# A routed expert layer: the up product with its weights as the stationary side, fetched per tile from DRAM

## The chip, the cores and the metric

The kernel runs on one core of a Trainium2 chip. The metric is the device time of one launch in microseconds, the median over runs. The engines of the core are TensorE (PE, with its weight loads in a row of its own, PEld), VectorE (DVE), ScalarE (ACT), GpSimd (POOL) and SyncE (SP, which here only issues DMAs). All arithmetic is fp32. In this trace one fp32 product stands as two matmul records, a transpose as one.

## The reference, cut to what matters

The network takes `u` of shape (8, 512, 128) through eight residual blocks: a rotating state-space layer, a feed-forward layer, a four-layer linear-attention encoder, the feed-forward layer again, causal attention with its own feed-forward, a mixture of experts, a gated linear attention, and the mixture of experts once more with the same weights. Each block reads a layer norm of the stream and adds its result. The block that matters is the mixture of experts, with 8 experts, 128 features, 352 hidden units, and two experts for each token:

```python
xn = rms_norm(x, norm_scale)
scores = jnp.einsum('bsd,ed->bse', xn, w_router)
_, ids = jax.lax.top_k(scores, 2)
c = jnp.take_along_axis(jax.nn.softmax(scores, axis=-1), ids, axis=-1)
h = jnp.einsum('bsd,ehd->bseh', xn, w_up)          # 704 = 2 * 352 columns
val, gate = jnp.split(h, 2, axis=-1)
h = val * jax.nn.silu(gate)
y = jnp.einsum('bseh,edh->bsed', h, w_down)
yk = jnp.take_along_axis(y, ids[..., None], axis=2)
out = jnp.sum(yk * c[..., None], axis=2) + x
```

## The kernel before

All blocks are recorded into one list of operations, each with the engines that can do it, a planned cost, the operations it depends on and a rank. A planner in the kernel (`Flow.run`) then goes through the list: at each step it takes the operation that can start first by its own planned times, and of equals the one of lowest rank. The result is a fixed order on every engine, written out by `Flow.emit`. The rank of an operation is the age of its thread plus the TensorE cost that the thread has recorded so far (`f.turn(thread, age)`). So the three constants at the end, `FIRST` (ages of the eight sequences in the first five blocks), `LATER` and `AGES` (ages of the threads of the last three blocks), decide which thread goes first where several could. The lag of an operation is how long after its end the planner lets its readers start. SP's queue is ordered in the same way, and each engine works through its queue strictly in order.

The last three blocks work on two halves of four sequences each. For each half and each of the two mixtures there are four threads. *Enter* makes the normed rows, writes them to DRAM (`rows_in`) and computes the scores. *Route* (`moe_route`) sorts the 4096 token-expert pairs of the half into 39 tiles (`TILES`) of 128 rows, one expert for each tile, and leaves three lists of integers: `h.get` (the rows to gather), `h.put` (where each result goes) and `h.off` (the column at which the tile's expert begins). *Experts* (`moe_experts`) does the tiles, 156 in all four passes. *Combine* loads the scattered rows back (`moe_combine`, line 2091) and adds the two results of each token to the stream. Between the two mixtures stands the gated attention of the half (`gated_steps`).

A tile goes like this. An indirect DMA on POOL gathers 128 rows (line 1983). Four tiles are transposed into one PSUM bank, and one operation scales them into `xt`. `wide` reads the tile's offset into a register of TensorE and does two products with `xt` as the stationary side: the gate (line 2018) and the value (line 2019), each 352 columns wide, from the expert's weights, which all eight experts hold on chip in `room_m` (8 x 1088 words a partition: 704 up, 384 down). Tanh on ScalarE and two operations on VectorE make the activation `g`, 128 tokens by 352 units. Three transposes through the identity and one copy turn it into `gt`. `deep` (line 2028) does three products with `gt` as stationary side and the down weights moving, 128 columns each. After four tiles the result is scaled, and an indirect DMA on POOL scatters each tile's rows (line 1993). There are three buffers for `g` and two for `gt`, `xr`, `xt` and `yr`. Their names in the trace are only `left` and `right`, the two areas of SBUF, and nearly all operations are recorded at lines 216 and 231.

Of the kernel before, what the change touches and what calls it, by code (L numbers as in the profile page):

```python
# [12 lines left out]
I32 = mybir.dt.int32  # L13
AF = mybir.ActivationFunctionType
ALU = mybir.AluOpType
# [5 lines left out]
P = 128  # L21
B = 8
S = 512
D = 128
NT = S // P
HALVES = 2
# [3 lines left out]
TILES = (2 * B * S // HALVES + 8 * (P - 1)) // P  # L30
# [648 lines left out]
def f_copy(f, out, in_):  # L679
    f.either(("scalar", "copy", (out, in_), {}), ("vector", "tensor_copy", (out, in_), {}))  # L680
# [10 lines left out]
class EncLane:  # L691

    WORDS = 3968

# [127 lines left out]
class FrontLane:  # L822

    WORDS = 4136

# [923 lines left out]
class MoeLane:  # L1749

    N = HALVES * NT
    WORDS = 0

    def __init__(self, base, ints):
        n, e = B // HALVES * NT, 8
        lane = Lane(base)
        self.r, self.by = lane.take(8, n, e), lane.take(3, e, n)
        self.high = lane.take(2 * n, TILES, at=0)
        self.m, self.full, self.q = lane.take(8, n), lane.take(e, n), lane.take(4, e)
        self.c = lane.take(2, n)  # L1760
        self.own = self.by.rearrange("p a e t -> p (a e t)")[:, 0 : TILES * e].rearrange("p (i e) -> p i e", e=e)
        self.ex, self.src = lane.take(TILES), lane.take(TILES)
        self.bits = [(LnBits(lane), lane.take(2, NT), lane.take(NT)) for i in range(B // HALVES)]
        self.get, self.put = ints[:, 0:TILES], ints[:, TILES : 2 * TILES]
        self.off = ints[0:1, 2 * TILES : 3 * TILES]
        self.saves, self.gathers, self.puts, self.loads, self.written = [], [], [], [], []

    @staticmethod
# [5 lines left out]
class ExpertLane:  # L1774


    def __init__(self, base, xn, y, low):
        lane = Lane(base)
        self.xn, self.y, self.low = xn, y, low
        self.zt = [lane.take(S) for i in range(2)]  # L1780
        self.xr, self.xt = [lane.take(4, D) for i in range(2)], [lane.take(4, P) for i in range(2)]
        self.g, self.gt = [lane.take(3 * P) for i in range(3)], [lane.take(3, P) for i in range(2)]
        self.yr = [lane.take(4, D) for i in range(2)]
        self.turn = {}

    WORDS = 1024 + 2048 + 1152 + 768 + 1024

    def next(self, name):
        i = self.turn[name] = self.turn.get(name, -1) + 1
# [4 lines left out]
def scaled(f, out, in_, by):  # L1794
# [1 line left out]
        ("scalar", "activation", (out, in_, AF.Copy), dict(scale=by)),  # L1796
        ("vector", "tensor_scalar", (out, in_, by, None, ALU.mult), {}),
    )


def moe_ready(k, f, box):

    for g in box.g:
        f.gpsimd.memset(g, 0.0)


def moe_enter(k, f, w, b, h, box):
# [38 lines left out]
def moe_route(k, f, w, half, h, box):  # L1846
# [66 lines left out]
        ALU.is_ge,  # L1913
    )
    v.tensor_reduce(h.ex[0:1], h.own[0:1], AX.X, ALU.add)
    v.tensor_scalar(h.ex[0:1], h.ex[0:1], float(E - 1), float(ROW), ALU.min, ALU.mult)
    v.tensor_copy(off, h.ex[0:1])
    v.tensor_tensor(e, s, wide(0), ALU.subtract)
    f.scalar.activation(e, e, AF.Exp)
    v.tensor_reduce(m[:, 1, :], e, AX.X, ALU.add)  # L1920
# [51 lines left out]
def moe_experts(k, f, w, half, h, box):  # L1972

    HID, ROW, E = 352, 1088, 8
    nc, tc = k.nc, k.tc
    xs, ys, off = k.rows_in[half], k.rows_out[half], h.off
    before, saved, h.gathers, h.puts, h.saves = h.loads, h.saves, [], [], []
    k.turn_of += 1
    group, written = f"rows{k.turn_of}", []
    h.written = written  # L1980

    def get(x, i):
        return lambda: nc.gpsimd.indirect_dma_start(  # L1983
            out=x.real(),
            out_offset=None,
            in_=xs,
            in_offset=bass.IndirectOffsetOnAxis(ap=h.get[:, i : i + 1].real(), axis=0),
        )

    def put(y, i):  # L1990

        def emit():
            made = nc.gpsimd.indirect_dma_start(  # L1993
                out=ys,
                out_offset=bass.IndirectOffsetOnAxis(ap=h.put[:, i : i + 1].real(), axis=0),
                in_=y.real(),
                in_offset=None,
            )
            if written:
                tc.declare_no_dep(made.ins, group=group, reason="no two of them write the same row")  # L2000
                tc.add_manual_dep(made.ins, written[0].name, SYNC, reason="what it overwrites")
            tc.add_to_no_dep_group(group, made.ins)
            written.append(made.ins)

        return emit

    def wide(i, held, pg, pv, xt, experts):

        def emit():
            o = held[i] = nc.values_load(  # L2010
                off[0:1, i : i + 1].real(),
                engines=[mybir.EngineType.PE],
                min_val=0,
                max_val=(E - 1) * ROW,
                skip_runtime_bounds_check_because="clamped where it is made",
            )
            all_of = experts.real()
            nc.tensor.matmul(pg.real(), xt.real(), all_of[:, bass.ds(o + HID, HID)], start=True, stop=True)  # L2018
            nc.tensor.matmul(pv.real(), xt.real(), all_of[:, bass.ds(o, HID)], start=True, stop=True)  # L2019

        return emit

    def deep(i, held, py, gt, experts):

        def emit():
            o, all_of = held[i], experts.real()
            for q in range(3):
                nc.tensor.matmul(  # L2028
                    py.real(),
                    gt[:, q, :].real(),  # L2030
                    all_of[:, bass.ds(o + 2 * HID + q * D, D)],
                    start=(q == 0),
                    stop=(q == 2),
                )

        return emit

    held = {}
    experts = w["experts"]
    for first in range(0, TILES, 4):  # L2040
        m = min(4, TILES - first)
        xr, xt, yr = box.next("xr"), box.next("xt"), box.next("yr")
        for j in range(m):
            i = first + j
            h.gathers.append(
                f.op([("gpsimd", 1.26, get(xr[:, j, :], i), None)], [h.get[:, i : i + 1]], [xr[:, j, :]], after=saved, lag=2.2)
            )
        pt, py = f.ps([P, 4, P]), f.ps([P, 4, D])
        for j in range(m):
            f.tensor.transpose(pt[:, j, :], xr[:, j, :], k.ident)  # L2050
        scaled(f, xt[:, 0:m, :], pt[:, 0:m, :], k.col["m_ns"])
        for j in range(m):
            i = first + j
            g, gt = box.next("g"), box.next("gt")
            pg, pv = f.ps([P, HID]), f.ps([P, HID])
            f.op([("tensor", 1.27, wide(i, held, pg, pv, xt[:, j, :], experts), None)], [xt[:, j, :], off, experts], [pg, pv])
            f.scalar.activation(g[:, 0:HID], pg, AF.Tanh, scale=0.5)
            f.vector.scalar_tensor_tensor(g[:, 0:HID], g[:, 0:HID], 1.0, pg, ALU.add, ALU.mult)
            f.vector.tensor_tensor(g[:, 0:HID], g[:, 0:HID], pv, ALU.mult)
            pt = f.ps([P, 3, P])  # L2060
            for q in range(3):
                f.tensor.transpose(pt[:, q, :], g[:, q * P : (q + 1) * P], k.ident)
            f_copy(f, gt, pt)
            f.op([("tensor", 0.68, deep(i, held, py[:, j, :], gt, experts), None)], [gt, experts], [py[:, j, :]])
        if first + m < TILES:
            scaled(f, yr[:, 0:m, :], py[:, 0:m, :], 0.5)
        for j in range(m):
            i = first + j
            if first + m == TILES:
                scaled(f, yr[:, j, :], py[:, j, :], 0.5)  # L2070
            h.puts.append(
                f.op(
                    [("gpsimd", 1.26, put(yr[:, j, :], i), None)],
                    [yr[:, j, :], h.put[:, i : i + 1]],
                    [],
                    after=before + h.puts[:1],
                    lag=2.2,
                )
            )

# [296 lines left out]
def both_blocks(k, saved, out):  # L2377
# [6 lines left out]
    with tc.tile_pool(name="net", bufs=1) as one:  # L2384
# [97 lines left out]

        some, other = cut(left), cut(right)
        f.turn("load", -1000.0)
        room_m = some(8 * 1088)
        y = [shaped(some(4 * D), (2, 2, D)) for i in range(2)]
        room_g, room_head = some(2338), some(304)
        hs = [MoeLane(some(MoeLane.words()), some(3 * TILES + 3).bitcast(I32)) for i in range(HALVES)]
        rows = [shaped(some(NT * D), (NT, D)) for i in range(2)]
        room_x = some(ExpertLane.WORDS)  # L2490
        pairs = [GatedLane(other(GatedLane.WORDS)) for i in range(2)]
        kept = other(GATED_FOLD)
        low = [shaped(other(4 * P), (4, P)) for i in range(2)]
        w = f.load(k, "m", room_head, only=("wr", "rev", "before", "iota", "dest"))
        w |= f.load(k, "m", room_m, parts=8, only=("experts",))
        wg = f.load(k, "g", room_g)
        box = ExpertLane(room_x, rows, y, low)
        f.turn(("route", 0, True), LATER + AGES[0])
        moe_ready(k, f, box)

        age = [LATER + a for a in AGES]

        def moe(half, first, then, out=None):
# [38 lines left out]
            f.emit(tiles)  # L2542


LATER = 700.0


AGES = [-33.0, -19.0, -149.0, -22.0, 62.0, 85.0, 147.0, -119.0, 102.0, -157.0]


FIRST = [30.0, 66.0, 62.0, 89.0, 185.0, 190.0, 210.0, 220.0, 327.0]


@with_exitstack
# [275 lines left out]
```

## Time and profile before

| what | value |
|---|---|
| median of 9 runs (lowest to highest) | 1644.92 us (1641.38 to 1649.53) |
| the profiled execution: its time, its span | 1644.99 us, 1643.3 us |
| mean granted clock of TensorE | 0.976 |
| the two up products (lines 2018 and 2019), 312 records each | 479 and 469 ns mean of a record |
| the three down products (line 2028), 936 records | 279 ns mean of a record |
| indirect gathers and scatters on POOL | 156 each, mean 1002 and 1010 ns |
| gather, from its issue to landing | 2.6 us median (2.4 to 3.6) |
| DMA over the span | 54.26 MB, 33 GB/s |

The span runs from the first to the last instruction, and the profiled execution's own time is 1.7 us longer. A row of a group gives its engine, its operation, what it writes and reads, its count, its busy time, the mean of one in ns, and the idle time ahead of it with what ended that. TensorE's matmuls overlap and their ends are modelled, so the distance between starts says more than a duration. Idle time of an engine that is not the bound costs nothing.

### The profile page before, as it was taken

The page shows a single profiled execution, that of the slowest core. Times are in us where ns is not written, and L with a number is a line of the kernel's source. Part 1 is how long each engine was busy: PE and PEld are TensorE (multiplying, and loading weights), DVE is VectorE, ACT ScalarE, POOL GpSimd, SP SyncE. Part 2 cuts the span into 40 slices and gives each one's busy share as a digit, 9 for nine tenths or more (in the row PEclk, how much of TensorE's full clock was granted, in tenths as well). Part 3 has the DMA queues.
Part 4 walks back from the last instruction along what each step waited for, and adds up shares of the span by engine and source line. Part 5 has one row for each costly group of instructions (what it writes and reads, how often), then busy time and mean ns, then how long its engine had stood idle before and what let it go on. Part 6 is the DMA issues. An engine that isn't in the chain of part 4 may idle for free.

```text
span 1643.3 us, 29385 instructions
## 1 busy us (share of the span) xinstructions
PE 1554.2 (95%) x10231; PEld 1105.4 (67%) x10231; DVE 1095.2 (67%) x3413; ACT 926.1 (56%) x1824; POOL 839.3 (51%) x976
## 2 busy tenths in 40 slices
PE   4899999999999999999999999999999999999894
PEld 2567866767567576687566556787558875687773
DVE  7588656658756567567576753576986769976453
ACT  1466566556665656656667756545744357454452
POOL 4375344455444544435444465657245572556773
PEclk9899999999999999999999999999989999999997
DMA  6000000000000000001003010113001130012334
GB/s 222 1 1 1 1 1 8 2 1 8 1 1 8 1 8 1 1 19 44 1 28 108 14 26 28 43 38 99 14 20 38 37 99 14 20 40 44 83 95 104
DMA packets 40546, 54.26 MB, mean 33 GB/s; under 512 B 7012, under 2 KB 32101, under 8 KB 40135
## 3 DMA queue, kind: packets, MB, share of 16 engines
q1 hardware_dynamic: 21400, 26.62, 5.2%
q0 software_dynamic: 10256, 21.38, 5.1%
q10 hardware_dynamic: 8736, 4.29, 0.8%
q8 instruction: 86, 1.41, 0.4%
q14 instruction: 68, 0.56, 0.1%
HBM read 33.52 MB, written 18.61 MB: 32 GB/s over the span
## 4 chain that ended last, share of the span: by engine, by line


## 5 line engine op out<-in xcount | busy, mean ns | idle before, releaser
L216 PE MATMUL ps_w<-left 128*128 128x128 f32 (+3 forms) x2540 | 450.7, 322 | 7.0 <-DVE left L216 5.7
L216 PEld LDWEIGHTS ps_w<-left 128*128 128x128 f32 x2540 | 332.4, 193 | 100.0 <-issue 64.1
L216 PE MATMUL ps_w<-right 128*128 128x128 f32 (+2 forms) x1656 | 348.6, 351 | 20.6 <-DVE right L216 13.3
L216 PEld LDWEIGHTS ps_w<-right 128*128 128x128 f32 x1656 | 225.9, 196 | 97.3 <-issue 55.1
L216 ACT ACTIVATE right<-ps_w 128x512 f32<-128x512 f32 (+1 forms) x394 | 206.8, 597 | 92.3 <-PE ps_w L231 74.8
L216 ACT ACTIVATE left<-ps_w 128x352 f32<-128x352 f32 (+2 forms) x307 | 157.3, 519 | 137.0 <-PE ps_w L216 58.5
L216 ACT COPY left<-ps_w 128x384 f32<-128x384 f32 (+3 forms) x268 | 128.1, 489 | 163.8 <-PE ps_w L216 141.2
L231 PE MATMUL ps_w<-right 128*32 128x512 f32 (+9 forms) x2256 | 202.7, 444 | 9.0 <-DVE right L216 5.6
L216 DVE SCALAR_TENSOR_TENSOR left<-left,ps_w 128x352 f32<-128x352 f32 (+1 forms) x220 | 122.7, 563 | 124.7 <-ACT left L216 124.1
L1993 POOL DMA_INDIRECT rows_out<-left x156 | 157.6, 1010 | 80.4 <-ACT left L216 38.2
L1983 POOL DMA_INDIRECT left<-rows_in,left x156 | 156.3, 1002 | 66.8 <-issue 28.9
L216 PE MATMUL ps_w<-w_ident,left 128*128 128x128 f32 x1072 | 178.1, 282 | 6.3 <-DVE left L216 4.1
L216 DVE TENSOR_TENSOR left<-left,ps_w 128x352 f32<-128x352 f32 (+2 forms) x228 | 125.9, 553 | 76.6 <-PE ps_w L216 57.6
L216 PEld LDWEIGHTS ps_w<-w_ident,left 128*128 128x128 f32 x1072 | 131.6, 145 | 58.7 <-issue 23.3
L216 POOL TENSOR_SCALAR_AFFINE_SELECT right<-right 128x512 f32<-128x512 f32 x129 | 82.1, 650 | 167.2 <-ACT right L216 157.8
L231 PEld LDWEIGHTS ps_w<-right 128*32 128x32 f32 (+3 forms) x2256 | 84.6, 150 | 103.4 <-issue 53.0
L2028 PEld LDWEIGHTS ps_w<-left 128*128 128x128 f32 x936 | 122.5, 193 | 27.2 <-ACT left L216 5.4
L2028 PE MATMUL ps_w<-left 128*128 x936 | 129.1, 279 | 3.4 <-ACT left L216 2.9
L2018 PE MATMUL ps_w<-left 128*128 x312 | 123.8, 479 | 2.7 <-ACT left L216 2.6
L216 POOL TENSOR_TENSOR left<-left,mhalf 128x4 f32<-128x4 f32 (+1 forms) x96 | 112.3, 1172 | 17.4 <-DVE left L216 11.8
L2019 PE MATMUL ps_w<-left 128*128 x312 | 120.7, 469 | 0.0
L216 POOL TENSOR_TENSOR left<-left 128x512 f32<-128x512 f32 x64 | 84.7, 1326 | 40.1 <-ACT left L216 31.8
(114 smaller groups left out, 2187.5 us busy)
## 6 DMA issues: line engine op xcount, KB each, us to landing
left<-rows_out SPq DMA_DIRECT2D x24, 256.0 KB
left<-in_m_dram SPq DMA_DIRECT2D x8, 544.0 KB
rows_in<-left ACTq DMA_DIRECT2D x16, 256.0 KB
left<-in_e_dram SPq DMA_DIRECT2D x4, 850.0 KB
left<-rows_in,left POOLq DMA_INDIRECT x156, 2.6
rows_out<-left POOLq DMA_INDIRECT x156, 2.3
x<-in_u_dram SPq DMA_DIRECT2D x8, 256.0 KB
saved<-x SPq DMA_DIRECT2D x8, 256.0 KB
```

Of the source, the lines that this page charges most:

```text
L216: return lambda: getattr(host, method)(*[real(v) for v in args], **{n: real(v) for n, v in kw.items()})
L231: getattr(host, method)(*[real(v) for v in args], **{n: real(v) for n, v in kw.items()})
L1983: return lambda: nc.gpsimd.indirect_dma_start(out=x.real(), out_offset=None, in_=xs, in_offset=bass.IndirectOffsetOnAxis(ap=h.get[:, i : i ...
L1993: made = nc.gpsimd.indirect_dma_start(out=ys, out_offset=bass.IndirectOffsetOnAxis(ap=h.put[:, i : i + 1].real(), axis=0), in_=y.real(), i ...
L2018: nc.tensor.matmul(pg.real(), xt.real(), all_of[:, bass.ds(o + HID, HID)], start=True, stop=True)
L2019: nc.tensor.matmul(pv.real(), xt.real(), all_of[:, bass.ds(o, HID)], start=True, stop=True)
L2028: nc.tensor.matmul(py.real(), gt[:, q, :].real(), all_of[:, bass.ds(o + 2 * HID + q * D, D)], start=(q == 0), stop=(q == 2),)
```

## The change

The up product is turned round. The expert's up weights become the stationary side, in six pieces of up to 128 columns, and the 128 tokens of `xt` the moving side. The product comes out with hidden units on partitions, so tanh and the two operations on VectorE write `gt` directly, 384 columns wide (the third piece has 96 valid rows; `deep` reads only those). The transposes, the copy, the buffers `g` and their memsets go. The up weights no longer lie on chip: each tile's 704 columns are fetched from DRAM into one of eight buffers, by a DMA from SP whose offset SP reads from `h.off`. Only the down weights stay, 8 x 384 words. `h.off` holds two lists now, one for the fetch and one for `deep`, which reads its register itself. `gt` has four buffers. The planned lag of gathers and scatters goes from 2.2 to 4.0, and `LATER`, `AGES` and `FIRST` have new values.

```diff
-        self.g, self.gt = [lane.take(3 * P) for i in range(3)], [lane.take(3, P) for i in range(2)]
+        self.gt, self.up = [lane.take(3, P) for i in range(4)], [lane.take(704) for i in range(8)]
...
-    v.tensor_scalar(h.ex[0:1], h.ex[0:1], float(E - 1), float(ROW), ALU.min, ALU.mult)
-    v.tensor_copy(off, h.ex[0:1])
+    for i, step in enumerate((ROW, 3 * D)):
+        v.tensor_scalar(h.src[0:1], h.ex[0:1], float(E - 1), float(step), ALU.min, ALU.mult)
+        v.tensor_copy(off[:, i * TILES : (i + 1) * TILES], h.src[0:1])
...
-    def wide(i, held, pg, pv, xt, experts):
...
-            nc.tensor.matmul(pg.real(), xt.real(), all_of[:, bass.ds(o + HID, HID)], start=True, stop=True)
-            nc.tensor.matmul(pv.real(), xt.real(), all_of[:, bass.ds(o, HID)], start=True, stop=True)
+    def fetch(i, up):
...
+                engines=[mybir.EngineType.SP],
...
+            nc.sync.dma_start(up.real(), k.drams["m"][:, bass.ds(o + k.offsets["m"]["experts"][0], 2 * HID)])
...
-            g, gt = box.next("g"), box.next("gt")
-            pg, pv = f.ps([P, HID]), f.ps([P, HID])
-            f.op([("tensor", 1.27, wide(i, held, pg, pv, xt[:, j, :], experts), None)], [xt[:, j, :], off, experts], [pg, pv])
-            f.scalar.activation(g[:, 0:HID], pg, AF.Tanh, scale=0.5)
-            f.vector.scalar_tensor_tensor(g[:, 0:HID], g[:, 0:HID], 1.0, pg, ALU.add, ALU.mult)
-            f.vector.tensor_tensor(g[:, 0:HID], g[:, 0:HID], pv, ALU.mult)
-            pt = f.ps([P, 3, P])
-            for q in range(3):
-                f.tensor.transpose(pt[:, q, :], g[:, q * P : (q + 1) * P], k.ident)
-            f_copy(f, gt, pt)
-            f.op([("tensor", 0.68, deep(i, held, py[:, j, :], gt, experts), None)], [gt, experts], [py[:, j, :]])
+            gt, up = box.next("gt"), box.next("up")
+            f.op([("sync", 1.2, fetch(i, up), None)], [off[:, i : i + 1]], [up], lag=3.4)
+            pg, pv = f.ps([P, 3, P]), f.ps([P, 3, P])
+            for ps, at in ((pg, HID), (pv, 0)):
+                rows = [min(P, 2 * HID - at - q * P) for q in range(3)]
+                f.several(
+                    "tensor",
+                    0.68,
+                    [
+                        ("matmul", (ps[0 : rows[q], q, :], up[:, at + q * P : at + q * P + rows[q]], xt[:, j, :]), dict(start=True, stop=True))
+                        for q in range(3)
+                    ],
+                )
+            f.scalar.activation(gt, pg, AF.Tanh, scale=0.5)
+            f.vector.scalar_tensor_tensor(gt, gt, 1.0, pg, ALU.add, ALU.mult)
+            f.vector.tensor_tensor(gt, gt, pv, ALU.mult)
+            f.op([("tensor", 0.68, deep(i, py[:, j, :], gt, down), None)], [gt, off[:, TILES + i : TILES + i + 1], down], [py[:, j, :]])
...
-        room_m = some(8 * 1088)
+        room_m = some(8 * 3 * D)
...
-LATER = 700.0
-AGES = [-33.0, -19.0, -149.0, -22.0, 62.0, 85.0, 147.0, -119.0, 102.0, -157.0]
-FIRST = [30.0, 66.0, 62.0, 89.0, 185.0, 190.0, 210.0, 220.0, 327.0]
+LATER = 793.0
+AGES = [-5.0, -19.0, -197.0, 16.0, 62.0, 46.0, 290.0, -35.0, 52.0, -19.0]
+FIRST = [30.0, 66.0, 62.0, 89.0, 185.0, 190.0, 210.0, 217.0, 277.0]
```

The ten `AGES` belong, in order, to: enter and route of half 0, its experts, the gated attention of half 0, enter and route of half 1, its experts, the second enter and route of half 0, its experts, the gated attention of half 1, the second enter and route of half 1, its experts.

## The prediction

> **What bounds the kernel now.** I read the page's busy shares first, then the busy time by stage, then the spacing of instructions inside one expert tile, then the queues.
>
> ```profile
> PE 1554.2 (95%) x10231; PEld 1105.4 (67%) x10231; DVE 1095.2 (67%) x3413; ACT 926.1 (56%) x1824; POOL 839.3 (51%) x976
> ```
>
> TensorE looks like the bound, but a share is an average over stages. The cuts below are chosen by the trace: 950 is just ahead of the first gather (957.7), 1498.9 is the first gather of the last expert pass, 1624 is the end of its last scatter.
>
> ```profile
> 60.00:950.00 890.00, 873.34 (x6077) 601.32 (x6076) 591.36 (x1990) 555.02 (x1078) 416.63 (x532) 1.00 0.04 12
> 950.00:1498.90 548.90, 533.43 (x3377) 391.40 (x3374) 398.26 (x1099) 296.25 (x584) 309.88 (x313) 0.97 0.15 40
> 1498.90:1624.00 125.10, 116.09 (x685) 91.73 (x683) 58.70 (x131) 59.79 (x126) 90.00 (x93) 0.98 0.29 75
> 1624.00:1643.30 19.30, 0.00 (x0) 0.00 (x0) 8.67 (x32) 0.00 (x0) 0.00 (x0) 0.50 0.59 170
> ```
>
> The columns are the stretch, its length, the busy time of PE, PEld, DVE, ACT and POOL, the granted clock, the DMA share and GB/s. From 60 to 1498.9 TensorE is busy 1406.8 of 1438.9 us: whatever is taken off it there shortens the span, and only 32.1 us of idle time is left for a better order. The third stretch is another case: POOL shows 90.0 us of 125.1, but its 93 instructions are all indirect DMAs, and each is followed by dead time:
>
> ```profile
> 1526.24 0.98 POOL L1993 DMA_INDIRECT rows_out<-left  x1 [2.25 <-ACT left L216]
> 1527.52 0.96 POOL L1993 DMA_INDIRECT rows_out<-left  x1 [0.30 <-issue]
> 1615.35 0.96 POOL L1993 DMA_INDIRECT rows_out<-left  x1 [4.57 <-ACT left L216]
> ```
>
> A new one starts every 1.27 us (0.97 and a gap of 0.30 that is there even when nothing is waited for). 93 x 1.27 = 118.1 of 125.1 us: POOL bounds the last pass, and the other 7.0 us is three waits for scaled results (2.25, 4.57 and one of 0.98, each less 0.30). The last 19.3 us are final loads, adds and stores that the change does not touch.
>
> **The change, part by part.** First TensorE, per tile. Matmul durations overlap, so I take starts:
>
> ```profile
> 1564.40 0.49 PE L216 MATMUL ps_w<-w_ident,left 128*128 128x128 f32 x3
> 1564.72 0.76 PE L2018 MATMUL ps_w<-left 128*128 x2
> 1565.32 0.76 PE L2019 MATMUL ps_w<-left 128*128 x2
> 1565.91 0.83 PE L2028 MATMUL ps_w<-left 128*128 x6
> 1566.58 0.76 PE L2018 MATMUL ps_w<-left 128*128 x2
> ```
>
> Three transposes take 0.32, the two 352-wide up products 0.60 and 0.59, the three 128-wide down products 0.67: 2.18 us. The new up product is six products 128 wide with six different stationary operands; the down products are exactly that form, 0.67 for three. New tile: 9 x 0.67/3 = 2.01 us. It saves 0.17 us a tile, 26.5 us over 156 tiles. The 96-column and 96-row pieces I take at the same price, since the moving side is still 128 wide.
>
> By stage: the L2018 rows put 108 tiles ahead of 1498.9 and 48 behind it, so 18.4 us goes ahead and 8.2 us in the last pass. The built order also shifts work: behind the last routing product stood 49 up and 51 down products, now 47 and 48. Two up (1.34 each) and three down (0.67 each) move forward, 4.7 us. Ahead of 1498.9 the saving is 18.4 - 4.7 = 13.7 us.
>
> The last pass loses 8.2 + 4.7 = 12.9 us on TensorE (116.1 to 103.2), but POOL sets it. From its first gather on, the order now has 39 gathers, 39 own scatters and 11 left over from the other half: 89 instead of 93, 113.0 us. Of the 7.0 us of waits I keep half, since the products behind them are done sooner. 125.1 becomes 116.5: 8.6 us.
>
> Now the other engines.
>
> ```profile
> L2018 PE MATMUL ps_w<-left 128*128 x312 | 123.8, 479 | 2.7 <-ACT left L216 2.6
> L2028 PE MATMUL ps_w<-left 128*128 x936 | 129.1, 279 | 3.4 <-ACT left L216 2.9
> L216 ACT COPY left<-ps_w 128x384 f32<-128x384 f32 x145 | 68.1, 479 | 99.0 <-PE ps_w L216 80.8 <-DVE left L216 11.7 <-issue 2.8
> ```
>
> The first two rows count (two records for each fp32 product). The copy behind the transposes goes: 68.1 us of ScalarE and 11 copies on VectorE. Tanh and both VectorE operations grow from 352 to 384 columns: by the 512-column rows (597 against 467 ns, 679 against 516) that is 26 and 33 ns, 4 us of ScalarE and 10 us of VectorE over all tiles, hidden under TensorE, or in the last pass under POOL (VectorE 58.7 of 125.1). A tile's chain gets 0.32 + 0.48 us shorter. Two more tiny VectorE operations in each of four routings cost 0.17 to 0.29 each by the smallest VectorE rows (BATCH_NORM_AGGREGATE, 128x4 SCALAR_TENSOR_TENSOR), 1.4 to 2.3 us; they lie on the routing chain, under other products in three of four: I take 1. The three memsets and the smaller weight load (8 x 192 KB instead of 8 x 544 KB, landing before the first gather) cost and gain nothing that is waited for.
>
> The new wait is the fetch. The first up product of a tile waits for 704 x 4 x 128 = 360 KB, and all of TensorE's queue stands behind it.
>
> ```profile
> 0.00:30.00 30.00, 11.93 (x32) 7.48 (x32) 22.87 (x101) 3.52 (x6) 11.20 (x25) 1.00 0.88 304
> ```
>
> The opening loads move 304 GB/s at a share of 0.88, so 345 GB/s at full share: a fetch occupies all DMA engines for 1.04 us. Landing is bounded by the gather below (2.6 us median for 64 KB) and above by the final loads, 3.7 us from the first issue (1625.37) to the first add (1629.07) with eight in the queue; I take 3.5. It is covered by eight buffers, at 2.0 us or more a tile. At a pass's start it is covered too: the expert numbers are there before the last routing products (64 records), which the trace spreads over 8 us. SP issues the fetches in order with the combine loads, and those wait:
>
> ```profile
> SPq L2091 <- DMA rows_out<-left: 625.1, 14, 182.9
> SPq L2091 <- DVE right L216: 18.5, 12, 2.2
> SPq L2091 <- DMA left<-rows_out: 10.1, 6, 2.8
> ```
>
> The first load of a combine waits for all scatters of its half, and later fetches stand behind it. The trace issues those at 1129.8, 1334.6 and 1546.2, when 45, 84 and 126 tiles had begun; the new order has 49, 87 and 133 fetches ahead of these loads. The cover is 4, 3 and 7 tiles, 7 us or more at 2.5 us a tile, against 3.5. Exposed: bounds 0 and, if that cover is gone, the 45 us of the slower rival; I take 1, since the cover is twice the landing. A gain from fetching I exclude: data on chip cannot come late.
>
> A page rule speaks against the transfer size: the Trainium skill, DMA: Bandwidth & Descriptors, section Bandwidth, asks for 1 MiB or more a DMA to pass 75% of peak, and fits a fixed 2 us for each in its anatomy section. By its fit (an estimate from that page) a fetch takes 2.8 us; hidden behind eight buffers it leaves the sum as it is.
>
> The sum, against the profiled execution (span 1643.3, its own time 1644.99; the median of the runs, 1644.92, is the same): 1645.0 - 13.7 - 8.6 + 1 + 1 = 1624.7. Forecast **1625 us**. All ages change, so the order changes from about 100 us on; I count nothing for that, and 10 us either way in the range (a third of the 32.1 us idle).
>
> **Rivals.**
>
> *The whole gain and more.* Three banks a tile become two and the chain is shorter, so the order can also close gaps: all 26.5 us, and 7 us of the waits or idle: 1612. For it: TensorE's 98% up to 1498.9. Against: POOL's 1.27 us raster in the last pass.
>
> *The order gives it back.* The new ages leave TensorE idle 16 us longer than the 32.1 us: 1641, no change. For it: every engine's order differs. Against: idle time is low under the old order with more banks in use.
>
> *Fetches come late: slower.* Where combine loads and fetches alternate on SP (fetches 49 to 58, 87 to 95, 133 to 149, 33 in all) each fetch can be held by the load ahead, which waited (18.5 + 10.1)/24 = 1.2 us in the trace: 33 x 1.2 = 40 us, and 5 us for two uncovered starts: 1670. It decides from 20/33 = 0.6 us a fetch. For it: DMA load. The last pass has 0.29 already and 48 fetches add 0.40; around the combine loads (1546 to 1570, 0.58 at 164 GB/s) the sum is 0.98. Against: the cover above, and scatters that landed within 3.8 us at worst under that load.
>
> The trace shows the clock drop when TensorE starves (0.50 in the last stretch). The Trainium skill, TensorE: Matmul & The Clock Gate, in its part on HAM oscillation, says idle gaps above 3.4 us halve the clock for the next window; by it each late fetch of that length would cost some 1.7 us more (an estimate), making this rival 1670 and up.
>
> **How the numbers follow.** Chances: forecast 0.46 (1615 to 1635), the whole gain 0.18 (1600 to 1615), given back 0.11 (1635 to 1650), late fetches 0.25 (1648 and up). A measurement of this kernel can tell about 0.2%, 3.3 us, from no change: 1641.6 to 1648.2. Faster: 0.46 + 0.18 + 0.04 of the third = 0.68; same: 0.07; slower: 0.25. The range 1604 to 1660 leaves out 0.05 below and some 0.15 above.
>
> **What would show it.** Right: transposes gone but for the gathered rows and three up groups at 0.67 each half; TensorE some 26 us less busy; the last gather pass starting near 1485; POOL every 1.27 us in the last pass, which lasts about 117. Wrong: TensorE waiting for the fetched tile (DMA from the expert pack) above 20 us in all; indirect DMAs landing above 5 us; idle time before 1485 well over 32 us; a last pass under 110 us, or up products spaced wider than 0.23 us.

## The result, and the profile after

The change makes the kernel slower: 1653.27 us (median of 20 runs, 1645.08 to 1658.9) against 1644.66 us of the kernel before (62 runs beside it). The ratio is 1.0048, 95% interval 1.0032 to 1.0063. The forecast was 1625. The profiled execution after took 1649.62 us, 3.7 less than the median, so its trace holds only part of the loss: a span of 1647.9 us, against 1643.3.

The busy shares first. The first line of the page after:

```profile
PE 1536.8 (93%) x11011; PEld 1157.5 (70%) x11011; DVE 1098.0 (67%) x3411; ACT 872.0 (53%) x1680; POOL 833.9 (51%) x975
```

TensorE is busy 17.4 us less than before (1554.2), and yet the span is 4.6 us longer. So its time without work has grown by 22.0 us, from 89.1 to 111.1. Where it grew is told by the busy time by stage, cut at the first gather, the first gather of the last pass and the end of its last scatter (columns as in the table of before):

```profile
60.00:977.90 917.90, 893.43 (x6201) 612.60 (x6201) 596.73 (x2010) 565.85 (x1099) 414.97 (x534) 0.99 0.04 12
977.90:1503.60 525.70, 505.73 (x3848) 422.18 (x3847) 395.73 (x1083) 255.24 (x477) 311.48 (x314) 0.98 0.42 117
1503.60:1628.80 125.20, 106.87 (x878) 103.15 (x875) 59.16 (x127) 37.67 (x74) 85.60 (x89) 0.93 0.61 185
1628.80:1647.90 19.10, 0.00 (x0) 0.00 (x0) 8.76 (x32) 0.00 (x0) 0.00 (x0) 0.53 0.56 172
```

From 60 us to the last pass TensorE is idle 44.4 us (24.5 + 20.0, of 1443.6) where it was 32.1, and the last pass starts at 1503.6 instead of 1498.9. The last pass has 89 indirect DMAs, as counted ahead, but takes 125.2 us and not 116.5; TensorE is idle for 18.3 us of it, and the granted clock is 0.93 where it was 0.98.

What the tile costs is seen where TensorE works without a stall; what the last pass loses is seen right behind. TensorE's timeline after:

```profile
1558.00 5.61 PE L231 MATMUL ps_w<-left 128*128 128x128 f32 x48 [0.31 <-DMA left<-in_m_dram]
1563.44 2.84 PE L2029 MATMUL ps_w<-left 128*128 x24
...
1575.33 3.04 PE L2029 MATMUL ps_w<-left 128*128 x12 [2.27 <-DVE left L216]
...
1579.81 0.33 PE L216 MATMUL ps_w<-w_ident,left 128*128 128x128 f32 x1 [1.23 <-DMA left<-rows_in,left]
1587.18 0.48 PE L216 MATMUL ps_w<-w_ident,left 128*128 128x128 f32 x1 [7.04 <-DMA left<-rows_in,left]
1588.27 0.48 PE L216 MATMUL ps_w<-w_ident,left 128*128 128x128 f32 x1 [0.62 <-DMA left<-rows_in,left]
1589.53 5.49 PE L231 MATMUL ps_w<-left 128*128 128x128 f32 x24 [0.78 <-ACT left L216]
...
1601.35 2.89 PE L231 MATMUL ps_w<-left 128*128 128x128 f32 x24
```

The 48 records of four tiles' up products (three products for gate and three for value, two records each) start at 1558.00 and the next group at 1563.44: 0.113 us a record, 0.68 for three products. At 1579.81 TensorE transposes one gathered tile (L216, through `w_ident`), and the next comes 7.04 us later. The 24 records that follow take 5.28 us from start to start, where the same 24 take 2.72 at 1601.35: the granted clock is 0.50 from 1582.0 to 1595.7.

Why the tile came late stands in POOL's timeline of the same stretch:

```profile
1551.78 0.97 POOL L1978 DMA_INDIRECT left<-rows_in,left  x1 [0.30 <-issue]
1553.06 0.98 POOL L1988 DMA_INDIRECT rows_out<-left  x1 [0.31 <-issue]
...
1574.49 0.96 POOL L1988 DMA_INDIRECT rows_out<-left  x1 [0.30 <-issue]
1575.76 0.97 POOL L1978 DMA_INDIRECT left<-rows_in,left  x1 [0.30 <-issue]
1579.33 0.98 POOL L1988 DMA_INDIRECT rows_out<-left  x1 [2.60 <-ACT left L216]
...
1584.40 0.99 POOL L1978 DMA_INDIRECT left<-rows_in,left  x1 [0.30 <-issue]
```

Between the gathers at 1551.78 and 1575.76 stand 17 scatters in a row, 24 us in which no new tile is gathered. Then one gather, four scatters, of which the first waits 2.60 us for its result, and the next gather at 1584.40, for which TensorE waits until 1587.18. Scatter waits for product, product for gather, gather stands behind scatter.

Ahead of the last pass, TensorE's waits between 978 and 1503.6 (what waited, for what; sum, times, longest) show new rows:

```profile
PE ps_w L231 <- ACT left L216: 3.6, 5, 1.0
PE ps_w L216 <- DMA left<-in_m_dram: 3.0, 1, 3.0
PE ps_w L2029 <- DVE left L216: 2.7, 6, 0.8
```

The first and the third are 6.3 us on a tile's own chain: the up product waits for the scaled rows, the down product for `gt`. Before, two rows of the down product held 1.1 us there:

```profile
PE ps_w L2028 <- ACT left L216: 0.6, 2, 0.5
PE ps_w L2028 <- DVE left L216: 0.5, 1, 0.5
```

The middle row names the expert pack, but what waited is a transpose of gathered rows, and its weight load, at the same moment, names the gather:

```profile
1329.19 0.94 POOL L1978 DMA_INDIRECT left<-rows_in,left  x1 [0.30 <-issue]
...
1334.75 0.18 PEld L216 LDWEIGHTS ps_w<-w_ident,left 128*128 128x128 f32 x1 [3.23 <-DMA left<-rows_in,left]
1334.75 0.48 PE L216 MATMUL ps_w<-w_ident,left 128*128 128x128 f32 x1 [3.04 <-DMA left<-in_m_dram]
```

That gather landed 5.5 us after its issue, the longest landing of a gather in the trace, and e4_searched has a wait of 3.0 us at the same place that is put down to a gather. For the expert pack TensorE waits once in the whole run: 0.31 us at 1558.00, with 0.5 on the weight load beside it.

The page's DMA issues give the landing times:

```profile
left<-rows_in,left POOLq DMA_INDIRECT x156, 3.9
rows_out<-left POOLq DMA_INDIRECT x156, 3.6
```

A gather lands in 3.9 us (median) where it took 2.6, a scatter in 3.6 (2.3), beside 107.73 MB in all instead of 54.26. Both traces have the landing of only 19 gathers and 20 scatters of 156.

### The profile page after: what moved, and what is told of

The parts are those of the page before. It is cut to its first block, busy times and chain, and to the rows that moved or that the text cites. A ratio compares the mean times of both kernels' runs of the same rounds, so it can differ in the third digit from the quotient of the medians.

```text
span 1647.9 us, 31261 instructions
## 1 busy us (share of the span) xinstructions
PE 1536.8 (93%) x11011; PEld 1157.5 (70%) x11011; DVE 1098.0 (67%) x3411; ACT 872.0 (53%) x1680; POOL 833.9 (51%) x975
## 2 busy tenths in 40 slices
DMA packets 63019, 107.73 MB, mean 65 GB/s; under 512 B 9508, under 2 KB 35621, under 8 KB 62599
## 4 chain that ended last, share of the span: by engine, by line
## 5 line engine op out<-in xcount | busy, mean ns | idle before, releaser
L216 PE MATMUL ps_w<-left 128*128 128x128 f32 (+2 forms) x2540 | 453.1, 323 | 10.4 <-DVE left L216 9.0
L216 PEld LDWEIGHTS ps_w<-left 128*128 128x128 f32 x2540 | 332.3, 193 | 99.5 <-issue 62.2
L216 PE MATMUL ps_w<-right 128*128 128x128 f32 (+2 forms) x1656 | 347.9, 350 | 24.1 <-DVE right L216 14.2
L216 ACT ACTIVATE left<-ps_w 128x384 f32<-128x384 f32 (+2 forms) x305 | 160.3, 531 | 260.6 <-PE ps_w L231 169.2
L216 PEld LDWEIGHTS ps_w<-right 128*128 128x128 f32 x1656 | 225.4, 195 | 99.3 <-issue 59.2
L216 ACT ACTIVATE right<-ps_w 128x512 f32<-128x512 f32 (+1 forms) x394 | 205.9, 598 | 97.4 <-PE ps_w L231 79.7
L231 PE MATMUL ps_w<-left 128*128 128x128 f32 x1872 | 240.4, 282 | 7.1 <-ACT left L216 6.1
L231 PEld LDWEIGHTS ps_w<-left 128*128 128x128 f32 x1872 | 225.6, 192 | 14.3 <-ACT left L216 8.7
L216 DVE SCALAR_TENSOR_TENSOR left<-left,ps_w 128x384 f32<-128x384 f32 (+1 forms) x220 | 127.2, 587 | 128.1 <-ACT left L216 125.8
L216 DVE TENSOR_TENSOR left<-left,ps_w 128x384 f32<-128x384 f32 (+3 forms) x228 | 130.3, 575 | 65.8 <-PE ps_w L216 51.7
L216 POOL TENSOR_SCALAR_AFFINE_SELECT right<-right 128x512 f32<-128x512 f32 x129 | 81.5, 645 | 178.2 <-ACT right L216 170.3
L2029 PE MATMUL ps_w<-left 128*128 x936 | 135.3, 285 | 7.8 <-DVE left L216 6.8
L2029 PEld LDWEIGHTS ps_w<-left 128*128 128x128 f32 x936 | 118.1, 194 | 19.5 <-DVE left L216 9.9
L216 PE MATMUL ps_w<-w_ident,left 128*128 128x128 f32 x604 | 108.2, 282 | 15.9 <-DMA left<-rows_in,left 8.9
L216 POOL TENSOR_TENSOR left<-left,mhalf 128x4 f32<-128x4 f32 (+1 forms) x96 | 112.7, 1175 | 19.8 <-DVE left L216 15.0
L216 PEld LDWEIGHTS ps_w<-w_ident,left 128*128 128x128 f32 x604 | 74.7, 144 | 52.2 <-issue 14.0
L216 ACT ACTIVATE left<-left 128x127 f32<-128x127 f32 (+1 forms) x191 | 81.7, 485 | 43.7 <-DVE left L216 43.3
L216 POOL TENSOR_TENSOR left<-left 128x512 f32<-128x512 f32 x64 | 84.0, 1314 | 36.0 <-ACT left L216 30.2
```

The costliest lines, as they stand in the source:

```text
L216: return lambda: getattr(host, method)(*[real(v) for v in args], **{n: real(v) for n, v in kw.items()})
L231: getattr(host, method)(*[real(v) for v in args], **{n: real(v) for n, v in kw.items()})
L2029: nc.tensor.matmul(py.real(), gt[0:r, q, :].real(), all_of[0:r, bass.ds(o + q * D, D)], start=(q == 0), stop=(q == 2))
```

## The experiments

Three theories, which the expectations call O, A and D. *Order* (O): the TensorE saving is real and the fetches are on time; the emitted order of this kernel spends the saving, in the last pass by gathers behind scatters. *Ages* (A): the new constants are bad in themselves. *Transfers* (D): twice the bytes slow gathers and scatters, and that is the loss. The readings from all traces stand in one table, in us: start of the first gather and of the last pass's first gather, the length from there to the last scatter's start, TensorE idle from 60 us to the last pass and from there to the last scatter's end, and the clock lost from 60 us to the last pass ((1 - granted clock) x length).

| kernel | first gather | last pass | its length | idle ahead | idle in it | clock lost ahead |
|---|---|---|---|---|---|---|
| before | 957.7 | 1499.0 | 123.9 | 32.2 | 8.9 | 17.1 |
| before, again | 957.7 | 1495.9 | 123.9 | 31.6 | 8.9 | 15.3 |
| after | 978.0 | 1503.7 | 124.1 | 44.4 | 18.3 | 18.7 |
| e1_after_old_ages | 978.0 | 1516.4 | 140.6 | 51.0 | 27.5 | 25.6 |
| e1_before_new_ages | 975.5 | 1525.0 | 141.7 | 46.4 | 10.4 | 41.4 |
| e1_thin_fetch | 979.5 | 1511.7 | 119.3 | 43.8 | 17.0 | 27.3 |
| e1_gathers_early | 978.5 | 1503.4 | 112.3 | 45.8 | 11.4 | 17.0 |
| e2_before_early | 957.7 | 1503.4 | 125.4 | 31.9 | 10.5 | 22.2 |
| e2_early_thin | 978.0 | 1507.6 | 111.7 | 42.1 | 10.9 | 25.6 |
| e2_early_twice | 978.9 | 1540.7 | 133.2 | 61.8 | 24.6 | 40.3 |
| e2_searched | 957.0 | 1501.5 | 114.3 | 42.8 | 10.6 | 20.3 |
| e3_before_searched | 958.6 | 1557.6 | 159.2 | 66.0 | 35.9 | 38.0 |
| e3_searched_other | 957.8 | 1605.5 | 160.7 | 99.0 | 38.8 | 75.1 |
| e4_searched | 954.8 | 1502.8 | 113.1 | 40.9 | 10.6 | 23.8 |
| e4_searched_other | 960.1 | 1501.5 | 114.8 | 42.3 | 11.6 | 25.3 |
| e4_before_searched | 961.0 | 1515.5 | 120.3 | 32.3 | 7.5 | 30.9 |

A row is one execution. "Before, again" is e4_before; it and e2_before_early have the same program ahead of the last pass as "before", and the three start that pass between 1495.9 and 1503.4. Less the lost clock, the starts are 1480.5 to 1482 in all three, so the lost clock accounts for their differences to within 1.5 us. (A clock lost while TensorE is idle costs nothing, so this is an upper bound of what it takes.)

**Transfers away (e1_thin_fetch).** The first eight fetches fill the buffers, the other 148 bring 8 of the 704 columns; the rest of a buffer keeps an earlier expert's weights. Same order, same instructions.

```diff
...
-            nc.sync.dma_start(up.real(), k.drams["m"][:, bass.ds(o + k.offsets["m"]["experts"][0], 2 * HID)])
+            full = len(fetched) < 8
+            fetched.append(i)
+            a, b = (0, 2 * HID) if full else (HID, HID + 8)
+            nc.sync.dma_start(up.real()[:, a:b], k.drams["m"][:, bass.ds(o + k.offsets["m"]["experts"][0] + a, b - a)])
```

> The first eight fetches are whole; every later one moves only 8 of the 704 columns of each partition, so the weights used are stale and the results are not the reference's. Every instruction stands where it stood in the changed kernel, on every queue, with the same waits. Theory D (the transfers: 56 MB more on the DMA engines hold the gathers and the fetched weights back): the gathers' landing falls from 3.9 to about 2.6 us, the last pass loses most of its 12 us of waits, and the time falls to 1625-1640. Theory O (the order): the gathers land sooner too, but what TensorE and POOL wait for stands behind other work in their queues, so the time stays at 1648-1654.

Measured: 1651.2 us, ratio 1.0023 (1.0001 to 1.0046). The interval overlaps that of the whole change (1.0032 to 1.0063). Without 99% of the fetched bytes of those 148 tiles, the kernel is still not faster than before, and TensorE is idle nearly as long (43.8 and 17.0 us). The transposes' waits for gathered rows ahead of the last pass fall from 3.0 to 0.9 us (2.3 in e2_early_thin below), those in the last pass stay (10.5, against 8.9). So the bytes are not the larger part of the loss; that they cost some us is within these intervals. How soon the gathers land is not in this trace, so that part of the expectation was not seen.

**Ages exchanged (e1_after_old_ages, e1_before_new_ages).** The changed kernel with the constants of before, and the kernel before with the new ones.

```diff
-LATER = 793.0
-AGES = [-5.0, -19.0, -197.0, 16.0, 62.0, 46.0, 290.0, -35.0, 52.0, -19.0]
-FIRST = [30.0, 66.0, 62.0, 89.0, 185.0, 190.0, 210.0, 217.0, 277.0]
+LATER = 700.0
+AGES = [-33.0, -19.0, -149.0, -22.0, 62.0, 85.0, 147.0, -119.0, 102.0, -157.0]
+FIRST = [30.0, 66.0, 62.0, 89.0, 185.0, 190.0, 210.0, 220.0, 327.0]
```

(and the other way round in the kernel before)

> The changed kernel with LATER, AGES and FIRST of the kernel before; planned costs and lags stay. Theory A (the new ages are what costs the time): 1625-1640, with the first gather back near 958 and the last pass starting near 1485. Theory D: the ages are irrelevant, 1650-1656. Theory O (ages fit only the code that they were chosen for): slower than the changed kernel by 10-30 us, 1663-1683, with a longer last pass.

> The kernel before with LATER, AGES and FIRST of the changed kernel; its tile code and lags stay. Theory D: no change to speak of, 1642-1650. Theories A and O: slower than before by 8-25 us, 1653-1670; A wants the loss of the front (first gather some 20 us later than 958), O wants it mostly in the passes.

Measured: 1680.01 us, ratio 1.0211 (1.0166 to 1.0256), and 1683.43 us, ratio 1.0216 (1.0174 to 1.0258). Each program with the other's ages takes 2% more than the kernel before (the changed one 1.6% more than with its own), the second kernel more than either theory had expected. Both lose most in the last pass (140.6 and 141.7 us in the table). The late first gather is not told by the ages alone: with the old ages the changed kernel still has it at 978.0. The ages are neither good nor bad in themselves: each set fits its own program better. The theory of bad ages falls.

**Gathers earlier in the last pass (e1_gathers_early).** The gathers of the fourth pass get a rank that is 20 lower; nothing else changes.

```diff
+        age = f.age
+        f.turn(f.thread, age - (EARLY if k.turn_of == 4 else 0.0))
         for j in range(m):
             i = first + j
             h.gathers.append(
...
+        f.turn(f.thread, age)
...
+EARLY = 20.0
```

> The changed kernel, in which the gathers of the last expert pass alone get a rank 20 lower, so that POOL's order takes them ahead of scatters that are ready at the same time. Everything ahead of the last pass stays in place. Theory O: the wait of TensorE for gathers behind 17 scatters (7.0 us at 1580-1587, at half clock behind it) goes, the last pass falls from 125 to 114-118 us, the time to 1641-1646. Theory D: the gathers land late wherever they stand, 1650-1655.

Measured: 1642.23 us, ratio 0.9974 (0.9949 to 0.9999). Its last pass by stage:

```profile
1503.30:1616.60 113.30, 102.02 (x878) 98.59 (x876) 57.91 (x127) 37.12 (x74) 86.19 (x89) 1.00 0.67 205
```

It starts where it started (1503.4), and takes 113.3 us: 89 DMAs at 1.27 us are 113.0. POOL's waits beyond its raster are gone, and so is the half clock (1.00). The profiled execution is the fastest of the twelve (1637.09 us), but e2_early_thin below shows the same short pass. By the medians this one edit is worth 11 us, more than the 8.6 us by which the change had made the kernel slower, and the last pass is 3 us shorter than even the forecast had it.

**The same edit elsewhere (e2_before_early, e2_early_thin).** On the kernel before, as a control, and together with the thin fetch (both edits as shown).

> The kernel before with the same edit: the gathers of its last pass ranked 20 earlier. Its order has at most 11 scatters in a row in that pass and those at its end, so theory O wants no change, 1641-1649; if ranking gathers first were a gain of its own, whatever the order, 1633-1640.

> The run with the gathers of the last pass ranked earlier, with all fetches but the first eight cut to 8 of 704 columns (stale weights). Theory O: 1638-1643, within 3 us of the same order with whole fetches (1642). Theory D: what is left of the loss is contention, 1622-1634.

Measured: 1646.95 us, ratio 1.0000 (0.9972 to 1.0027), and 1643.53 us, ratio 0.9974 (0.9951 to 0.9998). The edit is worth nothing on the kernel before, so it repairs something that the change brought. With it, thin and whole fetches give the same ratio, each to about 0.24%: at this size the bytes cost nothing that these runs can tell.

**Twice the transfers (e2_early_twice).** Behind each fetch SP issues a second one of 360 KB from DRAM to a place in DRAM that nobody reads.

```diff
...
             nc.sync.dma_start(up.real(), k.drams["m"][:, bass.ds(o + k.offsets["m"]["experts"][0], 2 * HID)])
+            n = len(fetched)
+            fetched.append(i)
+            nc.sync.dma_start(k.twin[n * P : (n + 1) * P, :], k.drams["m"][:, bass.ds(o + k.offsets["m"]["experts"][0], 2 * HID)])
```

> The run with the gathers of the last pass ranked earlier, in which SP issues behind each fetch a second transfer of the same 360 KB from the expert pack to a scratch tensor in DRAM that nobody reads: the DMA load of the fetches is doubled (and more, since it is written to DRAM). Theory O: the buffers cover it, 1641-1650. Theory D: each tile pays again what it pays now, 1660 or more, with gathers landing above 5 us.

Measured: 1692.75 us, ratio 1.0257 (1.0219 to 1.0294), far above what the theory of the order had expected. Its two last stages ahead of the end:

```profile
978.80:1540.60 561.80, 526.43 (x3839) 439.34 (x3838) 396.88 (x1082) 254.80 (x476) 312.05 (x314) 0.94 0.56 179
1540.60:1674.00 133.40, 109.70 (x886) 105.33 (x884) 57.75 (x127) 37.68 (x75) 84.94 (x89) 0.93 0.81 279
```

Within some 0.3%, transfers are free up to the present size, and doubling them costs 50 us. The DMA share of the last pass goes from 0.67 to 0.81, and the stage behind the first gather grows by 37 us. So the theory of the transfers is wrong at this size, and the margin is less than a factor of two. (Each of the added transfers also writes to DRAM, which the kernel's own fetches do not, and stands in SP's queue ahead of later fetches and loads; which of the two costs the time, or the load on the DMA engines itself, was not told apart. TensorE's waits in this trace name neither a fetch nor, above 1.4 us, a gather.)

**An order chosen for the new program (e2_searched).** The ages and a rank for the gathers of each pass were chosen anew by the plan that the kernel itself makes. Against e1_gathers_early:

```diff
-        f.turn(f.thread, age - (EARLY if k.turn_of == 4 else 0.0))
+        f.turn(f.thread, age - EARLY[k.turn_of - 1])
...
-EARLY = 20.0
+EARLY = [6.0, -8.0, 16.0, 27.0]
...
-AGES = [-5.0, -19.0, -197.0, 16.0, 62.0, 46.0, 290.0, -35.0, 52.0, -19.0]
-FIRST = [30.0, 66.0, 62.0, 89.0, 185.0, 190.0, 210.0, 217.0, 277.0]
+AGES = [-1.0, -19.0, -195.0, 19.0, 44.0, 81.0, 285.0, -24.0, 115.0, -15.0]
+FIRST = [30.0, 66.0, 62.0, 89.0, 185.0, 190.0, 210.0, 220.0, 274.0]
```

> The changed kernel with ages chosen anew by the kernel's own planner, and gathers ranked earlier or later by a constant for each pass; the tile code is the changed kernel's. Its planned order takes the first gather 15 us earlier than the changed kernel's and starts the last pass 2 us earlier. Theory O (the saving on TensorE is there and the order spent it): the front's idle time falls back towards the 16.7 us of the kernel before, the last pass lasts 112-116 us, time 1625-1638. Theory D (transfers): 1645-1655. If only the last pass matters and fronts are a matter of chance: 1638-1645.

Measured: 1633.69 us, ratio 0.9906 (0.9873 to 0.9939). This beats both kernels.

**Is that gain the change's, or any search's? (e3, then e4.)** The kernel before got the same freedom (ages and four gather ranks), the changed kernel a second set from another start.

```diff
...
+EARLY = [-16.0, -2.0, -18.0, -12.0]
-AGES = [-33.0, -19.0, -149.0, -22.0, 62.0, 85.0, 147.0, -119.0, 102.0, -157.0]
+AGES = [-130.0, -19.0, -153.0, -19.0, 62.0, 94.0, 147.0, -35.0, 184.0, -166.0]
-FIRST = [30.0, 66.0, 62.0, 89.0, 185.0, 190.0, 210.0, 220.0, 327.0]
+FIRST = [30.0, 66.0, 62.0, 89.0, 185.0, 190.0, 210.0, 220.0, 361.0]
```

(the kernel before; the second set of the changed kernel:)

```diff
...
+EARLY = [5.0, -1.0, -19.0, 18.0]
+AGES = [-42.0, -23.0, -418.0, 14.0, 91.0, -45.0, 437.0, -75.0, 61.0, -198.0]
+FIRST = [32.0, 66.0, 62.0, 89.0, 185.0, 190.0, 210.0, 220.0, 385.0]
```

> The kernel before with its ages and the rank of the gathers chosen anew, by the same procedure, over the same constants and for the same time as in the searched version of the changed kernel. If the searched version's gain belongs to the turned product (shorter TensorE work that a fitting order lets through), the old program, whose ages already fitted it, gains nothing: 1637 to 1650, ratio 0.996 to 1.003. If any program gains from a new search, this one does too: 1625 to 1636, ratio below 0.995, and the change itself is then worth nothing.

> The changed kernel with a second set of ages from another start of the same procedure (gathers earlier by 5, -1, -19 and 18). If the gain of the first searched version comes from an order that fits, a second fitting order gives about the same: 1628 to 1642, last pass 112 to 118, start of the last pass near 1500. If the first one was a lucky single order: 1643 to 1660.

Measured: 1735.84 us, ratio 0.9957 (0.9928 to 0.9985), and 1786.85 us, ratio 1.0246 (1.0203 to 1.0289). The kernel before itself took 1741.26 us on this chip, 6% more than on the others, and there the changed kernel with its second order loses 2.5% to it. That speaks against the gain. All three were run once more on another chip, beside an unchanged copy of the kernel before:

> The kernel before, unchanged, with a profile of its own beside the searched versions: where the kernel before took 1741 us, its own trace was not at hand. Ratio 1.0 by construction. If the machine is as in the first runs: 1640 to 1650 with a last pass of 125; if it is as in the last call: 1735 to 1750, the lost 95 us behind the first gather, and the trace says on which wait.

> The kernel before with ages and gather ranks chosen anew (the same kernel as the first control of this sort). If the searched version's gain belongs to the turned product: ratio 0.996 to 1.006 here. If any program gains from a new search: below 0.994.

> The searched version of the changed kernel once more, so that it and the searched version of the kernel before are timed against the same runs. If the turned product carries the gain: ratio 0.985 to 0.995, and below the searched kernel before by 0.005 or more. If the gain was that of one order on one machine: 0.996 or more.

> The changed kernel with the second set of ages once more. If any order that fits the program gains: ratio 0.985 to 0.998. If orders that look alike in the plan differ on the chip by more than the change is worth: above 1.01, with TensorE waiting behind the first gather for 30 us or more than in the searched version.

Measured: e4_before 1646.62 us, ratio 1.0012 (0.9987 to 1.0038); e4_before_searched 1648.46 us, 1.0032 (1.0005 to 1.0059); e4_searched 1637.17 us, 0.9942 (0.9918 to 0.9966); e4_searched_other 1637.01 us, 0.9959 (0.9939 to 0.9978). Here a new search gives the kernel before nothing (0.4% on the slow chip) and the changed kernel 0.4% to 0.9%, by two different orders and, for the first of them, on two chips. So on these two chips the turned product is worth some 7 to 15 us if the order fits, of the 20 that were forecast; on the slow chip its one order that was tried lost. Where it lies is seen in two stages of e4_searched, from its first gather on:

```profile
954.70:1502.70 548.00, 525.58 (x3953) 436.70 (x3954) 396.54 (x1089) 262.26 (x491) 320.36 (x321) 0.96 0.40 112
1502.70:1616.80 114.10, 103.51 (x878) 100.35 (x876) 58.72 (x127) 37.45 (x74) 85.92 (x89) 0.98 0.65 203
```

and in the same stages of e4_before:

```profile
957.60:1495.80 538.20, 523.12 (x3295) 385.85 (x3288) 396.75 (x1091) 291.53 (x576) 307.91 (x310) 0.98 0.15 41
1495.80:1620.70 124.90, 116.05 (x685) 91.80 (x683) 58.80 (x131) 59.59 (x126) 89.97 (x93) 0.98 0.29 75
```

The last pass is 10.8 us shorter (114.1 against 124.9). Four indirect DMAs fewer (89 against 93, 5.1 us) are a matter of the order: e4_before_searched also has 89, and 121.3 us (in an execution 8.5 us over its median), so the tile's own part is nearer 7. Ahead of the last pass no gain is seen: the three traces of the changed kernel's searched versions start it between 1501.5 and 1502.8, the three of the old order between 1495.9 and 1503.4. Less the lost clock they start it at 1476 to 1481, up to 5 us earlier than the old order (1480.5 to 1482), and the clock that they lose takes that back.

## Why the prediction was wrong, step by step

**Per tile: right.** Predicted 0.67 us for each three products and 2.01 a tile; measured 0.68 for three up products and 0.67 for three down products (48 records in 5.44 us, 24 in 2.68). By these spacings a tile takes 2.03 us where it took 2.18: 0.15 saved, 23 us over 156 tiles, where 26.5 were predicted. ScalarE is 54 us less busy, on no path.

**The fetch: right.** Its wait was put at 1 us on the path; TensorE waits 0.31 us for the pack (0.5 with the weight load), thin fetches gain 2 us by the medians, within the noise, and with the order mended none. SP's waits say that the fetches stand ahead of TensorE and wait for a free buffer:

```profile
SPq L2012 <- PE ps_w L231: 362.5, 102, 33.3
```

The rival that ended on the slower side, late fetches, had 0.25 and fell. The kernel is slower, but not by that mechanism. (The 2.8 us for a fetch rest on a fit that the page cited there gives for DMAs issued from GpSimd; SP issues these, no trace here has their landing, and the sum did not use it.)

**"I count nothing for the order": the step that failed.** It decided the sign, in two places.

*The last pass*: 116.5 predicted, 125.2 measured. The 89 DMAs at 1.27 us (113.0) were right. Half of the 7.0 us of waits was kept on the ground that products done sooner let scatters go sooner; measured were 12.2 us, because in this order the gathers stand behind 17 scatters. With 20 ranks off the gathers the pass is 113.3. The step took the raster from the new order, but not what stands in front of whom in it, though the built order was at hand.

*Ahead of the last pass*: -13.7 predicted, +4.7 measured; these 18 us are the larger part of the miss. TensorE's busy time went down by 7.6 (1406.8 to 1399.2), and its idle time up by 12.3. Part of that is this order: the first gather comes 20.3 us later than before, in code that the change did not touch, and idle time ahead of it goes from 16.7 to 24.5. But both searched orders have the first gather back at 955 to 960, and still 41 to 43 us of idle time, against 32 under the old order. Common to the orders of the new tile are two kinds of waits between the first gather and the last pass. The waits on a tile's own chain are 6.3 us after, 6.0 to 6.7 in e1_gathers_early and the searched versions, 5.5 in e1_thin_fetch, and 1.1 before. The transposes' waits for gathered rows are about 3 to 4 us, 0.9 and 2.3 in the two thin traces, and next to nothing before. The prediction put no wait on either: it counted the chain as shorter, and did not count that the work of TensorE that covers it is shorter as well, nor that gathers would land later (3.9 us against 2.6). That these waits are the cause is read from the traces and was not isolated by a run; how much of the 18 us is which stays open.

**The clock: a term that was missing.** From the start to the end of the last pass the lower clock costs 39.3 us after and 29.3 before (8.5 and 2.0 of it in the last pass). The difference lifts TensorE's busy time by up to 9.9 us; with the smaller saving a tile it covers the 9.1 us between the 17.4 that the page shows and the 26.5 predicted. In the last pass the 7.04 us gap and the half clock over and behind it (24 records in 5.28 us) are most of it. The Trainium skill, TensorE: Matmul & The Clock Gate, in its part on HAM oscillation, puts the threshold at about 3.4 us of idle time. The trace agrees for this gap, with 13.7 us of half clock from 1582.0, and its stretches of half clock are multiples of 3.4 us; but the clock also halves from 1575.2 to 1578.6, in the gap of 2.27 us ahead of 1575.33, and from 1104.2 to 1111.0, where TensorE had been busy for all of the 6.7 us before. So idle time isn't the only thing that lowers it here, and ahead of the last pass no run ties the lost clock to the change: it differs as much between traces of one order (15.3 to 22.2). The prediction cited the rule for one rival and left the clock out of its own sum; in the last pass its idle time was paid for twice.

**The rivals.** The nearest was "the order gives it back": 0.11, with 16 us of added idle time and no change as its result. Its mechanism was right and its size too small: 22.0 us of idle time and 9.9 us of clock. "The whole gain and more", 1612, fell with the forecast; even the best order stays 22 us above it. Of the prediction's signs of being wrong, the idle time came (44.4 us against 32.1), the wait for fetched tiles did not, and landings above 5 us came singly (gathers up to 5.5, scatters up to 6.9).

## What to carry to other kernels

Where a program's order is chosen by a plan, a change to the program is a change to the order, and the order can cost more than the change: here 2% by ages that fit the other program, against half a per cent for the change itself. Judge such a change with an order chosen anew for both sides, and read the built order of the queue that sets the end (who stands behind whom) before counting its raster. Where TensorE is the bound at 98%, work taken off it comes back as a shorter span only if what it waits for is early; here the rest turned into idle time, and in the last pass into a lower clock as well.

## What the hardware showed that was not expected

Twice the bytes cost nothing that these runs can tell (some 0.3%), three times the bytes 50 us: with the gathers early, 54.99 MB (thin fetches) and 107.73 MB (whole ones) give the same ratio, 0.9974; 164.00 MB give 1.0257, at a DMA share of 0.81 in the worst stage.

The same kernel took 5% longer on one chip than on another, all of it behind the first gather. The searched kernel before took 1735.84 us there and 1648.46 on the other; up to the first gather the traces agree (958.6 and 961.0), POOL's raster is 1.27 us in both, and the packets of the indirect DMAs take the same time (4.7% of 1736 us, 5.0% of 1655). The stages behind it, on the slower chip:

```profile
958.60:1557.50 598.90, 549.26 (x3312) 402.46 (x3306) 399.15 (x1095) 292.11 (x579) 310.28 (x314) 0.94 0.14 37
1557.50:1717.70 160.20, 124.41 (x666) 95.28 (x664) 57.57 (x127) 58.26 (x122) 85.74 (x89) 0.93 0.21 57
```

On the other chip they are 554.4 and 121.3 us. Scatters wait for their scaled results for 110.3 us in 28 waits (up to 11.5), where they wait 36.3 on the other chip. What starts it there stays open.
